# A graph attention stage's products and its edge setup: written one after the other, or in pieces between each other

## The chip, the cores and the metric

The kernel runs on one core of one Trainium2 chip. The core has five engines that run side by side: TensorE (PE, matrix products), VectorE (DVE), ScalarE (ACT), GpSimd (POOL) and SyncE (SP, which here only issues transfers). The metric is the time of one execution on the device, in microseconds (us); less is better.

## The reference, cut to what matters

Two graph layers over 6250 nodes with 256 features and 100000 edges, which come sorted by their destination. What matters here is the start of the first layer:

```python
h = jnp.maximum(_layernorm(x, axis=-1), 0.0)
Qh = (h @ Wq + bq).reshape(N, 8, 32)
Kh = (h @ Wk + bk).reshape(N, 8, 32)
Vh = (h @ Wv + bv).reshape(N, 8, 32)
s = jnp.einsum('nhc,nhc->nh', Qh, Kh) / sqrt(32)
# then, over the edges and one loop per node: a softmax by destination of leaky_relu(s[src] + s[dst]),
# a weighted sum of Vh[src], an output product, batch norm, a two-layer product, batch norm;
# then a second layer of three sums over neighbours, each with a product
```

So for each node a score per head (8) and a value row (256) are wanted before any edge can be worked on.

## The kernel before, in words

The kernel has stages that follow one another: setup of the edges, the QKV stage, attention over the edges, the two dense products with batch norm, and three stages that gather neighbours' rows. The change touches the first two, both in `gnn_kernel`.

**Edge setup** (lines 196 to 296). The edges are cut into 53 chunks of 15 x 128 places, and a chunk's edges lie in one partition at first. `srow` and `krow` (53 x 1920 and 53 x 1922, int32) are loaded from the lists of sources and destinations, `line`, `nodes`, `ahead` and `stop` for a check of the input. Then come, on VectorE if nothing else is said:

- `kf` (L234) and `base` (L238), casts to float; `loc` (L240), the destination less the chunk's first node; `sf` (L236) and `loc_h` (L242), casts on ScalarE; `loc_h` is stored by SP.
- `lst` (L245) and `fst` (L250), marks of the last and first edges of a node; `fst` is multiplied by -3e38 (L253) and stored through ScalarE's queue (`by_two`, L193).
- Three times fifteen transposes of 128 columns on TensorE (L259), of `sf`, `loc` and `lst`, eight and seven at a time into a tile `idx_tp`, and a copy of each batch (L260) into `src_t`, `loc_t` and `fst_t`, the tiles that the later stages index by chunk.
- The check (L264 to L296): two passes over `line` (125 x 800) and a dozen operations on one row; one product sums the counts, and `odd_i` receives the flag that picks the path after the QKV stage.

**QKV stage** (L299 to L344). The 6250 nodes are 50 blocks of 125 rows, in ten groups of five. A group's rows of `x` are loaded at once by SP into `xg` (two buffers). `layernorm` takes bn_stats and bn_aggr of each of the five blocks (L150, L151), then one square root on ScalarE (L141), one reciprocal and one product on VectorE (L142, L154). For each block: ScalarE makes `h0` (normalize and Relu, L320), TensorE transposes its two halves into `tp` (L323, two buffers), ScalarE copies them to `hb` (L325, three buffers) and issues its store to `h_d` (L326); TensorE multiplies `hb` with `w_qk` (L330) into `qk_ps` (two buffers) and with `w_v` (L332) into `v_ps` (one buffer). VectorE adds the biases (L334, L336), multiplies Q with K (L338) and sums by head (L341); SP stores the row `vs`, values and scores, to `vs_d` in two parts of 112 and 13 rows.

**What sets the order.** In these two stages a list scheduler picks, for each engine, what is ready by its own reckoning, with the order in the program as priority. Each engine then carries out its queue strictly in the order chosen, and an instruction that waits for a semaphore holds up all behind it on its engine; the transfers that ScalarE issues stand in ScalarE's queue. The attention stage, which isn't changed, does it otherwise: inside `tc.manual_schedule(engines={EN.PE, EN.DVE, EN.Activation})` the three engines named get their instructions in the order in which the program writes them, from a list (`PLAN`). Engines that are not named, SP and GpSimd, remain with the scheduler.

After the QKV stage all engines read the flag, and attention begins with gathers by GpSimd out of `vs_d`.

Of the kernel before, what the change touches and what calls it, by code (L numbers as in the profile page):

```python
# [29 lines left out]
I32 = mybir.dt.int32  # L30
# [57 lines left out]
def gnn_kernel(ctx: ExitStack, tc: tile.TileContext, a: dict, out: bass.AP):  # L88
# [106 lines left out]

    src, dst = a["src"], a["dst"]
    srow = cp.tile([NCK, CE], I32, name="srow")
    nc.vector.memset(srow[:, :BACK], 0)
    krow = cp.tile([NCK, CE + 2], I32, name="krow")
    nc.vector.memset(krow[:, : BACK + 1], -1)  # L200
    nc.vector.memset(krow[:, CE + 1 :], PADKEY)
    at_n = cp.tile([NCK, 1], I32, name="at_n")
    nc.vector.memset(at_n, NN - LASTW)
    for c0, c1 in ((1, 49), (49, NCK - 1)):
        at, n = c0 * STEP, c1 - c0
        nc.scalar.dma_start(srow[c0:c1, :], edges(src, at - BACK, n, CE))
        nc.sync.dma_start(krow[c0:c1, :], edges(dst, at - BACK - 1, n, CE + 2))
        nc.sync.dma_start(at_n[c0:c1, :], edges(dst, at, n, 1))
    nc.scalar.dma_start(srow[0:1, BACK:], edges(src, 0, 1, CE - BACK))
    nc.sync.dma_start(krow[0:1, BACK + 1 :], edges(dst, 0, 1, CE + 1 - BACK))  # L210
    nc.scalar.dma_start(srow[NCK - 1 :, :], edges(src, NE - CE, 1, CE))
    nc.sync.dma_start(krow[NCK - 1 :, : CE + 1], edges(dst, NE - CE - 1, 1, CE + 1))
    nc.vector.memset(at_n[0:1, :], 0)


    nc.vector.memset(nodes[:, 0:1], 0)
    nc.vector.memset(nodes[:, NCK - 1 : NCK], NN - LASTW)
    nc.vector.memset(nodes[:, NCK:], NN)
    nc.sync.dma_start(nodes[:, 1 : NCK - 1], each(dst, STEP))
    ahead = cp.tile([1, NCK], I32, name="ahead")  # L220
    nc.vector.memset(ahead[:, 0:1], -1)
    nc.sync.dma_start(ahead[:, 1 : NCK - 1], each(dst, STEP - BACK - 1))
    nc.sync.dma_start(ahead[:, NCK - 1 :], edges(dst, NE - CE - 1, 1, 1))
    stop = cp.tile([1, 1], I32, name="stop")
    nc.sync.dma_start(stop, edges(dst, STEP * (NCK - 1), 1, 1))
    line = cp.tile([125, 801], I32, name="line")
    nc.vector.memset(line[0:1, 0:1], -1)
    nc.scalar.dma_start(line[0:1, 1:], edges(dst, 0, 1, 800))
    nc.scalar.dma_start(line[1:113, :], edges(dst, 799, 112, 801, 800))
    nc.scalar.dma_start(line[113:, :], edges(dst, 799 + 112 * 800, 12, 801, 800))  # L230


    kf = cp.tile([NCK, CE + 2], FT, name="kf")
    nc.vector.tensor_copy(kf, krow)  # L234
    sf = cp.tile([NCK, CE], FT, name="sf")
    nc.scalar.copy(sf, srow)  # L236
    base = cp.tile([NCK, 1], FT, name="base")
    nc.vector.tensor_copy(base, at_n)  # L238
    loc = cp.tile([NCK, CE], FT, name="loc")
    nc.vector.tensor_scalar(loc, kf[:, 1 : CE + 1], base, None, op0=OP.subtract)  # L240
    loc_h = cp.tile([NCK, CE], BF, name="loc_h")
    nc.scalar.copy(loc_h, loc)  # L242
    by_two(nc.sync, loc_d, loc_h)
    lst = cp.tile([NCK, CK, P], FT, name="lst")
    nc.vector.tensor_tensor(  # L245
        lst.rearrange("c j e -> c (j e)"), kf[:, 2:], kf[:, 1 : CE + 1], op=OP.not_equal
    )
    nc.vector.memset(lst[:, :, P - 1 :], 1.0)
    fst = cp.tile([NCK, CK, P], FT, name="fst")
    nc.vector.tensor_tensor(  # L250
        fst.rearrange("c j e -> c (j e)"), kf[:, 1 : CE + 1], kf[:, :CE], op=OP.not_equal
    )
    nc.vector.tensor_scalar(fst, fst, -BIG, None, op0=OP.mult)  # L253
    by_two(nc.scalar, fst_d, fst)
    for of, to in ((sf, src_c), (loc, loc_c), (lst.rearrange("c j e -> c (j e)"), lst_c)):
        for j0, j1 in ((0, 8), (8, CK)):
            tp = cps.tile([P, 8, NCK], FT, name="idx_tp", bufs=2)
            for j in range(j0, j1):
                nc.tensor.transpose(tp[:, j - j0, :], of[:, j * P : (j + 1) * P], ident[:NCK, :NCK])  # L259
            nc.vector.tensor_copy(to[:, :, j0:j1].rearrange("p c j -> p j c"), tp[:, : j1 - j0, :])  # L260


    odd = cp.tile([P, 1], FT, name="odd")
    nc.vector.memset(odd, 0.0)  # L264
    fall = cp.tile([125, 800], FT, name="fall")
    nc.vector.tensor_tensor(fall, line[:, 1:], line[:, :800], op=OP.is_lt)
    nc.vector.tensor_reduce(odd[:125], fall, AX.X, OP.add)
    nodes_f = cp.tile([1, NCK + 1], FT, name="nodes_f")
    nc.vector.tensor_copy(nodes_f, nodes[:, : NCK + 1])
    ahead_f = cp.tile([1, NCK], FT, name="ahead_f")  # L270
    nc.vector.tensor_copy(ahead_f, ahead)
    bad = cp.tile([1, 3 * NCK + 2], FT, name="bad")
    nc.vector.tensor_copy(bad[:, 3 * NCK :][:, 0:1], stop)

    nc.vector.tensor_tensor(bad[:, :NCK], nodes_f[:, 1:], nodes_f[:, :NCK], op=OP.subtract)
    nc.vector.tensor_scalar(bad[:, :NCK], bad[:, :NCK], float(P), None, op0=OP.is_gt)
    nc.vector.tensor_tensor(bad[:, NCK : 2 * NCK], ahead_f, nodes_f[:, :NCK], op=OP.is_ge)
    told = cp.tile([1, NCK], FT, name="told")
    nc.vector.tensor_scalar(
        told, iota[0:1, :NCK], float(DONE[1] - DONE[0]), float(DONE[0]), op0=OP.mult, op1=OP.add  # L280
    )
    nc.vector.tensor_tensor(bad[:, 2 * NCK : 3 * NCK], nodes_f[:, :NCK], told, op=OP.is_lt)

    nc.vector.tensor_scalar(
        bad[:, 3 * NCK : 3 * NCK + 1], bad[:, 3 * NCK : 3 * NCK + 1], float(NN - LASTW), None, op0=OP.is_lt
    )
    nc.vector.tensor_scalar(
        bad[:, 3 * NCK + 1 :], nodes_f[:, NCK - 2 : NCK - 1], float(NN - P), None, op0=OP.is_gt
    )
    nbad = cp.tile([1, 1], FT, name="nbad")  # L290
    nc.vector.tensor_reduce(nbad, bad, AX.X, OP.add)
    nc.vector.tensor_tensor(odd[0:1], odd[0:1], nbad, op=OP.add)
    nodd = cps.tile([1, 1], FT, name="nodd")
    nc.tensor.matmul(nodd, odd, ones[:, 0:1], start=True, stop=True)
    odd_i = cp.tile([1, 1], I32, name="odd_i")
    nc.vector.tensor_copy(odd_i, nodd)  # L296


    with (  # L299
# [5 lines left out]
        w_v = weight(wp, "w_v", [a["L0_gnn_Wv"]])  # L305
        b_qk = wp.tile([P, 2 * D], FT, name="b_qk")
# [6 lines left out]
        for b0 in range(0, NFB, 5):  # L313
            xg = sp.tile([P, 5, D], FT, name="xg")
            halves(nc.sync, lambda s: xg[s], lambda s: rows_of(a["x"], b0, 5)[s])
            r, m = layernorm(sp, [xg[:FB, k, :] for k in range(5)], 5)
            for k in range(5):
                b = b0 + k
                h0 = sp.tile([P, D], FT, name="h0")
                nc.scalar.activation(h0[:FB], xg[:FB, k, :], AF.Relu, bias=m[:FB, k : k + 1], scale=r[:FB, k : k + 1])  # L320
                tp = pp.tile([P, 2, FB], FT, name="tp")
                for f in range(2):
# [1467 lines left out]
```

## Time and profile before

| | us |
|---|---|
| median of 14 runs | 4516.52 |
| lowest, highest | 4513.11, 4523.44 |
| the profiled execution | 4517.94 |
| its span, first to last instruction | 4516.2 |
| first product of the QKV stage starts | 30.26 |
| last group of products of the QKV stage starts | 183.40 |
| first gather of the attention stage starts | 190.89 |

A row of the order of time has the start in us, the duration in us, the engine, the line, the operation, the tiles written and read, the shapes, how many were merged, and in brackets the idle time ahead of it and what ended it. Merged rows ("x4") give the time from the first start to the last end. A matmul of this type counts twice in the records (the page's "x200" of L330 are 100 in the program). A row of the windows has, after the stretch, its length, the busy time of TensorE's matmuls, its weight loads, VectorE, ScalarE and GpSimd with their counts, the granted TensorE clock (1.00 is full), and the share and rate of the transfers. The page's rows of 40 digits are the span in equal slices of 113 us; "PEclk" is the granted clock in tenths. No clock is on record for the first 35 us; the rows show 1.00 there.

### The profile page before, as it was taken

The page shows a single profiled execution, that of the slowest core. Times are in us where ns is not written, and L with a number is a line of the kernel's source. Part 1 is how long each engine was busy: PE and PEld are TensorE (multiplying, and loading weights), DVE is VectorE, ACT ScalarE, POOL GpSimd, SP SyncE. Part 2 cuts the span into 40 slices and gives each one's busy share as a digit, 9 for nine tenths or more (in the row PEclk, how much of TensorE's full clock was granted, in tenths as well). Part 3 has the DMA queues.
Part 4 walks back from the last instruction along what each step waited for, and adds up shares of the span by engine and source line. Part 5 has one row for each costly group of instructions (what it writes and reads, how often), then busy time and mean ns, then how long its engine had stood idle before and what let it go on. Part 6 is the DMA issues. An engine that isn't in the chain of part 4 may idle for free. (4 is left out here: it accounts for less than half of the span.)

```text
span 4516.2 us, 36719 instructions
## 1 busy us (share of the span) xinstructions
PE 3647.8 (81%) x11051; PEld 1916.2 (42%) x11051; DVE 1486.1 (33%) x3034; ACT 746.1 (17%) x1610; POOL 3011.8 (67%) x3186
## 2 busy tenths in 40 slices
PE   7666666666696677888777899999999797888888
PEld 4344444444444333444333344444444333333333
DVE  6577777777724111111111121212121111111110
ACT  2244444444326000000000000000000000000000
POOL 0277777777300677777776777777776677777776
PEclk9888888888896788767777999999999656556655
DMA  4555555555205444444443777878776333333333
GB/s 126 146 150 152 152 152 153 152 152 152 69 0 159 147 126 126 126 126 126 127 126 115 221 244 231 244 232 244 232 243 205 100 112 112 112 112 112 113 112 105
DMA packets 315949, 671.18 MB, mean 149 GB/s; under 512 B 79412, under 2 KB 166734, under 8 KB 315743
## 3 DMA queue, kind: packets, MB, share of 16 engines
q0 software_dynamic: 178080, 524.47, 40.4%
q1 hardware_dynamic: 114005, 126.08, 9.2%
q10 hardware_dynamic: 23658, 18.21, 1.4%
q8 instruction: 89, 1.46, 0.1%
q14 instruction: 117, 0.96, 0.1%
HBM read 614.38 MB, written 54.13 MB: 148 GB/s over the span
## 5 line engine op out<-in xcount | busy, mean ns | idle before, releaser
L894 PE MATMUL sum<-g,hot 128*128 128x256 f32 (+1 forms) x4770 | 2276.2, 597 | 380.4 <-DMA g<-g_d,src_t 212.4
L396 POOL DMA_INDIRECT g<-g_d,src_t x1590 | 1505.6, 947 | 788.8 <-issue 522.8
L894 PEld LDWEIGHTS sum<-g,hot 128*128 128x128 f32 x4770 | 981.5, 240 | 1581.4 <-DMA g<-y_d,src_t 572.2
L396 POOL DMA_INDIRECT g<-vs_d,src_t x795 | 754.0, 948 | 431.6 <-issue 220.6
L396 POOL DMA_INDIRECT g<-y_d,src_t x795 | 751.6, 945 | 273.7 <-issue 219.5
L696 PE MATMUL acc<-g,hot 128*128 128x264 f32 x1590 | 513.9, 469 | 59.8 <-DVE g L686 58.6
L696 PEld LDWEIGHTS acc<-g,hot 128*128 128x128 f32 x1590 | 345.6, 234 | 125.2 <-DVE g L686 71.5
L413 DVE TENSOR_TENSOR hot<-ruler,loc_t 128x1920 f32<-128x1920 f32 x159 | 341.4, 2149 | 11.9 <-DMA g_d<-g 10.0
L1012 DVE TENSOR_TENSOR o<-sum,base 128x256 f32<-128x256 f32 (+1 forms) x53 | 22.5, 425 | 865.9 <-PE sum L894 865.9
L525 PE MATMUL flip<-ident,s_e 128*120 128x128 f32 x53 | 24.8, 468 | 339.5 <-ACT s_e L520 339.5
L686 DVE TENSOR_TENSOR g<-g,at_ps 128x1024 f32<-128x1024 f32 x212 | 239.2, 1150 | 15.4 <-ACT at_ps L677 9.4
L936 DVE SCALAR_TENSOR_TENSOR own<-own,eps,sum 128x256 f32<-128x256 f32 (+1 forms) x53 | 25.4, 480 | 522.2 <-PE sum L894 522.2
L966 PE MATMUL h_ps<-tt,g_w 128*128 128x512 f32 (+1 forms) x448 | 190.8, 570 | 0.6 <-ACT tt L954 0.6
L525 PEld LDWEIGHTS flip<-ident,s_e 128*120 128x120 f32 x53 | 9.3, 176 | 350.0 <-ACT s_e L520 350.0
L1000 DVE SCALAR_TENSOR_TENSOR own<-own,eps,sum 128x512 f32<-128x512 f32 (+1 forms) x53 | 39.5, 746 | 346.5 <-PE sum L894 346.5
L918 ACT COPY tt<-tp 128x256 f32<-128x256 f32 (+1 forms) x53 | 19.7, 372 | 733.0 <-PE tp L917 733.0
L925 DVE TENSOR_TENSOR g<-h_ps,g_b 128x512 f32<-128x512 f32 (+1 forms) x53 | 36.6, 691 | 305.2 <-issue 275.4
L954 ACT COPY tt<-tp 128x512 f32<-128x512 f32 (+1 forms) x53 | 31.0, 585 | 609.4 <-PE tp L953 609.4
L985 DVE SCALAR_TENSOR_TENSOR base<-y,eps,x 128x256 f32<-128x256 f32 (+1 forms) x53 | 25.5, 483 | 311.8 <-ACT y L980 310.6
L966 PEld LDWEIGHTS h_ps<-tt,g_w 128*128 128x128 f32 x448 | 82.7, 190 | 100.3 <-issue 99.5
L492 DVE TENSOR_TENSOR hot<-ruler,loc_t 128x1024 f32<-128x1024 f32 x106 | 117.2, 1145 | 5.5 <-ACT ruler L407 5.5
L506 ACT ACTIVATE hot_t<-loc_r,minus_p 128x896 bf16<-128x896 bf16 x106 | 115.6, 1091 | 9.9 <-DMA loc_r<-loc_d 9.9
(161 smaller groups left out, 2724.6 us busy)
## 6 DMA issues: line engine op xcount, KB each, us to landing
loc_r<-loc_d SPq DMA_DIRECT2D x53, 480.0 KB
g<-g_d,src_t POOLq DMA_INDIRECT x1590
g_d<-g SPq DMA_DIRECT2D x52, 256.0 KB
own<-g_d SPq DMA_DIRECT2D x52, 256.0 KB
g<-vs_d,src_t POOLq DMA_INDIRECT x795
g<-y_d,src_t POOLq DMA_INDIRECT x795
xg<-in_x_dram SPq DMA_DIRECT2D x20, 560.0 KB
own<-vs_d SPq DMA_DIRECT2D x52, 132.0 KB
```

The costliest lines, as they stand in the source:

```text
L396: nc.gpsimd.indirect_dma_start(out=to, out_offset=None, in_=table, in_offset=bass.IndirectOffsetOnAxis(ap=src_c[:, c, j : j + 1], axis=0),)
L413: nc.vector.tensor_tensor(hot, rule[:, None, :P].to_broadcast([P, CK, P]), loc_c[:, c, :][:, :, None].to_broadcast([P, CK, P]), op=OP.is_e ...
L492: nc.vector.tensor_tensor(s.hot[:, js, :], rule[:, None, :P].to_broadcast([P, n, P]), loc_c[:, s.c, js][:, :, None].to_broadcast([P, n, P] ...
L506: nc.scalar.activation(s.hot_t[:, edges_of(q)], s.loc_r[:, edges_of(q)], AF.Square, bias=minus_p)
L525: nc.tensor.transpose(s.flip[: CK * H, :P], s.s_e.rearrange("p j h -> p (j h)"), ident)
L686: nc.vector.tensor_tensor(rows, rows, s.w_e[:, j0 // 8, j0 % 8 : j0 % 8 + n, :, None].to_broadcast([P, n, H, C]), op=OP.mult,)
L696: nc.tensor.matmul(s.acc, s.hot[:, j, :], s.g[:, j, :], start=j == 0, stop=j == CK - 1)
L894: nc.tensor.matmul(ps, hot[:, j, :], g, start=j == 0, stop=j == CK - 1)
L925: nc.vector.tensor_tensor(g1[R], h_ps[R], g_b1[R], op=OP.add)
L954: nc.scalar.copy(tt[:, :, q, R], tp[:, :, R])
L966: nc.tensor.matmul(h_ps[:, :n], g_w2[:, k, f * P : (f + 1) * P], tt_f[:, k, :n], start=k == 0, stop=k == 3)
L1000: nc.vector.scalar_tensor_tensor(own[R], own[R], eps1[R, 1:2], ps[R], op0=OP.mult, op1=OP.add)
```

## The change

The edge setup becomes functions. `load_edges` holds all loads and memsets and is called after the weights, the first ten blocks of `x` and the biases have been asked for. The rest is a list of ten pieces, of which one is run after each block of products from the sixth on. `kf`, `base`, `loc` and the product of `fst` are on GpSimd. `layernorm` is taken apart: `statistics(b)` for a block of the next group stands ahead of the products of the present one, two, two and one of them in the first three blocks of a group. `turned(b + 1)` stands ahead of the products of block b. `xg` has three buffers, and SP issues the store to `h_d`. All of the loop is inside `tc.manual_schedule` for TensorE, VectorE and ScalarE.

```diff
-    (edge setup in one piece: loads, kf, sf, base, loc, loc_h, lst, fst, the transposes, the check)
+    def load_edges():
+        (all memsets and loads of srow, krow, at_n, nodes, ahead, stop, line, as before)
+    def destinations():
+        nc.gpsimd.tensor_copy(kf, krow)
+        nc.gpsimd.tensor_copy(base, at_n)
+        nc.gpsimd.tensor_scalar(loc, kf[:, 1 : CE + 1], base, None, op0=OP.subtract)
+        nc.scalar.copy(sf, srow)
+        loc_h = cp.tile([NCK, CE], BF, name="loc_h")
+        nc.scalar.copy(loc_h, loc)
+        by_two(nc.sync, loc_d, loc_h)
+    def last_edges():
+        nc.vector.tensor_tensor(lst..., kf[:, 2:], kf[:, 1 : CE + 1], op=OP.not_equal)
+        nc.vector.memset(lst[:, :, P - 1 :], 1.0)
+    def first_edges():
+        fst = cp.tile([NCK, CK, P], FT, name="fst")
+        nc.vector.tensor_tensor(fst..., kf[:, 1 : CE + 1], kf[:, :CE], op=OP.not_equal)
+        nc.gpsimd.tensor_scalar(fst, fst, -BIG, None, op0=OP.mult)
+        by_two(nc.scalar, fst_d, fst)
+    def flips(of, to):
+        (the transposes and the copy, as before; two pieces, of eight and of seven)
+    def check():
+        (as before)
+    edge_work = [
+        destinations,
+        check,
+        *flips(sf, src_c),
+        *flips(loc, loc_c),
+        last_edges,
+        *flips(lst.rearrange("c j e -> c (j e)"), lst_c),
+        first_edges,
+    ]
...
         w_qk = weight(wp, "w_qk", [a["L0_gnn_Wq"], a["L0_gnn_Wk"]])
         w_v = weight(wp, "w_v", [a["L0_gnn_Wv"]])
+        def load_x(b0):
+            xg = sp.tile([P, 5, D], FT, name="xg", bufs=3)
+            halves(nc.sync, lambda s: xg[s], lambda s: rows_of(a["x"], b0, 5)[s])
+            return xg
+        loaded = [load_x(0), load_x(5)]
...
         b_v = row(wp, "b_v", a["L0_gnn_bv"], D)
-        for b0 in range(0, NFB, 5):
-            xg = sp.tile([P, 5, D], FT, name="xg")
-            halves(nc.sync, lambda s: xg[s], lambda s: rows_of(a["x"], b0, 5)[s])
-            r, m = layernorm(sp, [xg[:FB, k, :] for k in range(5)], 5)
-            for k in range(5):
-                (h0, tp, hb, nc.scalar.dma_start to h_d, and the products)
+        load_edges()
+        mvs, norms = {}, {}
+        def statistics(b):
+            g, k = divmod(b, 5)
+            if k == 0:
+                mvs[g] = sp.tile([P, 5, 2], FT, name="ln_mv")
+            st = sp.tile([P, 6], FT, name="ln_st")
+            nc.vector.bn_stats(st[:FB], loaded[g][:FB, k, :])
+            nc.vector.bn_aggr(mvs[g][:FB, k, :], st[:FB])
+            if k == 4:
+                mv = mvs.pop(g)
+                r = rsqrt(sp, "ln_r", mv[:FB, :, 1], 5, FB)
+                m = sp.tile([P, 5], FT, name="ln_m")
+                nc.vector.scalar_tensor_tensor(m[:FB], mv[:FB, :, 0], -1.0, r[:FB], op0=OP.mult, op1=OP.mult)
+                norms[g] = r, m
+        def turned(b):
+            (h0 on ScalarE, two transposes into tp, hb on ScalarE, as before)
+            nc.sync.dma_start(h_d[:, :, b * FB : (b + 1) * FB], hb)
+            return hb
+        with tc.manual_schedule(engines={EN.PE, EN.DVE, EN.Activation}):
+            for b in range(5):
+                statistics(b)
+            nxt = turned(0)
+            for b in range(NFB):
+                g, k = divmod(b, 5)
+                for n in (2 * k, 2 * k + 1):
+                    if n < 5 and g + 1 < NFB // 5:
+                        statistics(5 * (g + 1) + n)
+                hb = nxt
+                if b + 1 < NFB:
+                    nxt = turned(b + 1)
+                if k == 4 and 5 * (g + 2) < NFB:
+                    loaded.append(load_x(5 * (g + 2)))
                 (the products of block b and VectorE's four operations, as before)
                 halves(nc.sync, lambda s: vs_d[b * FB : (b + 1) * FB, :][s], lambda s: vs[s])
+                if b > 4 and edge_work:
+                    edge_work.pop(0)()
```

Lines in brackets stand for code that is told in words.

## The prediction

> **What bounds the kernel now.** I read the page first, then the stage's waits, then its order of time, then the clock.
>
> ```profile
> span 4516.2 us, 36719 instructions
> PEclk9888888888896788767777999999999656556655
> ```
>
> The stages follow one another: GpSimd's first gather of the attention stage starts at 190.89 us, after the last products of the QKV stage, and the last matmul of that stage starts at 183.40. So whatever the QKV stage gains or loses moves the rest as a block. The profiled execution took 4517.94 us, 1.7 more than its span and 1.4 more than the median of the runs (4516.52).
>
> The stage's windows and its waits (30 to 185 us):
>
> ```profile
> 45.50:60.80 15.30, 14.81 (x51) 8.59 (x50) 11.06 (x33) 4.74 (x11) 0.00 (x0) 1.00 0.51 138
> ```
> ```profile
> PE qk_ps L330 <- ACT hb L325: 5.9, 24, 0.2
> ```
>
> In this group of five blocks TensorE is busy 14.81 of 15.30 us, VectorE 11.06, ScalarE 4.74: TensorE bounds the stage, and it waits mainly once in two blocks for a copy `hb`. The order of time gives the units:
>
> ```profile
> 27.50 0.30 ACT L141 ACTIVATE ln_r<-ln_mv,eps 125x5 f32<-125x5 f32 x1 [2.80 <-DVE ln_mv L151]
> 28.27 0.16 DVE L154 SCALAR_TENSOR_TENSOR ln_m<-ln_mv,ln_r 125x5 f32<-125x5 f32 x1
> 28.46 1.09 ACT L320 ACTIVATE h<-xg,ln_m,ln_r 125x256 f32<-125x256 f32 x2 [0.67 <-DVE ln_m L154]
> 29.12 0.29 PEld L323 LDWEIGHTS tp<-ident,h 125*128 125x128 f32 x2 [3.04 <-ACT h L320]
> 30.26 3.78 PE L330 MATMUL qk_ps<-w_qk,hb 128*125 128x512 f32 x4
> ...
> 181.68 1.88 PE L330 MATMUL qk_ps<-w_qk,hb 128*125 128x512 f32 x4
> 183.40 1.03 PE L332 MATMUL v_ps<-w_v,hb 128*125 128x256 f32 x4
> 183.59 0.69 DVE L334 TENSOR_TENSOR qk<-qk_ps,b_qk 125x512 f32<-125x512 f32 x1 [0.77 <-PE qk_ps L330]
> 184.66 0.41 DVE L336 TENSOR_TENSOR vs<-v_ps,b_v 125x256 f32<-125x256 f32 x1
> 185.00 0.41 DVE L341 TENSOR_REDUCE vs<-qk 125x8 f32<-125x256 f32 x1
> ```
>
> A block's products P take 1.72 us (181.68 to 183.40) plus 0.86 (`v` at 104.12, next transpose at 104.98) = 2.58; a block's two transposes T take 0.57 / 2 = 0.285. The scheduler's order repeats every 6.10 us for two blocks (98.67, 104.77), so 6.10 - 5.16 - 0.57 = 0.37 is waiting. The first block is slow: products from 30.26 to 35.32, 5.06 us, 2.5 over the usual.
>
> Is a written order kept even when its next instruction must wait? The attention stage has one, and there ScalarE shows:
>
> ```profile
> 460.76 0.41 ACT L772 COPY h_t<-h_own 128x256 f32 x1 [1.82 <-DVE stats L781]
> 461.07 1.04 ACT L506 ACTIVATE hot_t<-loc_r,minus_p 128x896 bf16<-128x896 bf16 x1
> ```
>
> The second has its row of `loc_r` loaded a chunk (19 us) earlier, yet stands 1.82 us behind the first, as listed. Nothing overtakes. The clock, in windows on its own grid of 3.41 us:
>
> ```profile
> 280.85:284.26 3.41, 0.23 (x3) 0.04 (x1) 3.05 (x9) 1.60 (x5) 2.61 (x3) 1.00 0.41 99
> 284.26:287.67 3.41, 0.81 (x3) 0.60 (x3) 0.90 (x3) 1.15 (x3) 2.50 (x4) 0.50 0.36 100
> 287.67:291.09 3.42, 3.42 (x16) 2.44 (x15) 2.56 (x9) 2.37 (x7) 2.54 (x3) 0.50 0.51 160
> 291.09:294.50 3.41, 2.45 (x25) 1.90 (x21) 2.80 (x8) 1.68 (x3) 2.77 (x3) 1.00 0.94 306
> ...
> 1390.18:1393.59 3.41, 1.73 (x16) 1.56 (x14) 2.06 (x6) 0.61 (x2) 0.00 (x0) 1.00 0.15 14
> 1393.59:1397.00 3.41, 1.97 (x6) 1.47 (x6) 0.65 (x4) 2.52 (x7) 0.00 (x0) 0.50 1.05 266
> ...
> 1738.34:1741.75 3.41, 2.04 (x6) 0.89 (x6) 0.00 (x0) 0.00 (x0) 2.80 (x3) 1.00 0.37 109
> 1741.75:1745.17 3.42, 1.74 (x6) 0.89 (x6) 2.02 (x2) 0.00 (x0) 2.50 (x4) 1.00 0.37 96
> ```
>
> The eighth field is the granted clock. A window with 0.23 us of TensorE work is followed by 0.50, so is one with 1.73 (a gap of 3.12 us began in it), so is 1741.75 (1.74); after 2.04 the clock held. It came back after a full window.
>
> **The change, part by part.** *Start: 13.1 us earlier.* `x` and weights now go out at 0.76 us. Traffic flowed from about 2 us and ran near 235 GB/s once queues were full (16 to 22 us: 216 to 250). The first `x` (625 KB) shares with the weights: 1.28 MB is 5.4 us, so about 8 us. Five statistics of 0.57 end near 11. But ScalarE itself issues three weight and eight edge loads ahead of its first square root, and in the run before its fourth issue went out only at 7.85, after earlier transfers had landed. Weights and `srow` (1.16 MB) with as much from SP are 10 us, so it is free near 12.1, plus the table load (1.28): 13.4. From the square root to the first product took 2.76 (27.50 to 30.26); the written order puts block 1's activation and T ahead of P(0), about 1.0 more. First product: 17.2 against 30.26. Ends: 14 and 20.
>
> *Steady order: 8.7 us less.* T(b+1) then P(b): 50 x 2.58 + 49 x 0.285 = 143.0, plus the slow first block 2.5 = 145.5. Before: 30.26 to 184.43 = 154.2. ScalarE no longer issues `h_d` (0.57 each); SP does: 0.57 + 0.32 + 0.39 for `vs_d` + 0.14 for `x` = 1.42 per block of 2.87, so it is hidden. If SP held `x` behind stores, each of eight groups would wait some 3 us (25 in all); before, `x` went out between stores, so I take nothing.
>
> *A new wait in each group: +28.8.* The fifth `statistics` of the next group stands in block k = 2 ahead of `turned(b+1)`, and contains a square root on ScalarE. So: VectorE must first finish block b-1, then bn_stats and bn_aggr; ScalarE waits with the square root; queued behind it is the activation of block b+1; TensorE waits with T(b+1), and P(b), ready, is behind that. From the end of P(b-1): 0.19 to VectorE (183.40 to 183.59), `vs` 0.41, `qk2` 0.35, reduce 0.45 = 1.40; bn_stats 0.34, bn_aggr 0.21 = 1.95; square root 0.33 = 2.28; activation 0.51 = 2.79; load 0.20 = 2.99. VectorE comes 0.2 to 0.3 late, since blocks 0 and 1 of a group carry two statistics (1.93 + 1.15 = 3.1 us against 2.87). I take 3.2, ends 3.0 and 3.5. Nine groups have a successor: 28.8.
>
> *Edge work in the stream.* It stood ahead of the products before, so its removal is in the start's term. Flips: 45 transposes of 0.117 (15 in 1.84, eight in 0.93) = +5.3 on TensorE; their copies (0.75 to 0.87) fit VectorE's slack in blocks 3 and 4. `check` after block 6: `fall` 0.96, its reduce 0.93, 14 small ones near 0.15 = 3.9, plus a matmul and a cast 0.6; it stands ahead of a k = 2 statistics, so all lengthens that wait: +4.5. `last_edges` after block 11, likewise: +2.2. `destinations`: `sf` and `loc_h` are 1.79 each on ScalarE, start 0.5 into P(5) and put the next activation at 4.5 where P ends at 2.6: +2.1. `first_edges` after block 14: reduce ends 1.40 after P, comparison 2.07, GpSimd's pass 1.85, two issues 0.62 on ScalarE's queue, behind them the activation 0.6 and 0.2: +6.8, all new.
>
> GpSimd's passes: no row shows one. iota took 232 ns for 128 columns and 127 for one, 0.83 ns a column, 1.7 us for 1920; the far end is a gather's 947 ns for 128 rows, 7.4 ns, 14.2 us. I take 1.7, an elementwise walk being nearest to iota. Then `kf` and `loc` end near 20 us, ScalarE asks at 41: hidden; at the far end they cost 3 there and 12.5 in `first_edges`. A gain is excluded, since VectorE has slack in the blocks concerned.
> The Trainium skill (GPSIMD Engine Reference, section 3.1) puts GpSimd near half of VectorE's elementwise rate, which speaks against moving work there; no run shows it, and by VectorE's 1.12 us pass it would make 2.2, 0.5 more in `first_edges`.
>
> *Clock: +19.* A gap of 3.2 us in windows of 3.41 nearly always leaves one window with over 1.6 idle, under 1.8 busy: a drop. Half clock lasts one window (loss 1.7) or two (loss up to 3.4, less the part that is gap). Averaged over where the gap falls, about 1.9. Nine groups plus `first_edges`: 10 x 1.9 = 19; ends 0 and 34.
> The Trainium skill (TensorE: Matmul & The Clock Gate, HAM oscillation) states "no PE-idle gaps >~3.4µs". By that rule nine gaps of 3.2 would be free, three long ones would drop, and the sum would be +33.6. The row at 1390.18, dropped with a gap of 3.12 us, disagrees, and I go by the row.
>
> Sum: -13.1 - 8.7 + 28.8 + 5.3 + 4.5 + 2.2 + 2.1 + 6.8 + 19 = +46.9. Against 4517.94: 4564.8, against the median 4563. After the stage nothing changes; I add nothing.
>
> **The rivals.** *The clock holds in the nine short gaps*, only those of `check`, `last_edges` and `first_edges` (6.8 to 7.7 and 5.4 us) dropping: 5.7 for 19, +33.6, 4550. For it: 1738.34 held at 2.04 busy. Against: 1390.18.
>
> *Faster: the written order doesn't bind*; T(b+1) and P(b) go ahead as they did before, where the square root (95.86) hid beside products. Then all waits (28.8 + 15.6 + 19 = 63.4) go: -13.1 - 8.7 + 5.3 = -16.5, 4500. It decides where the waits left total under 7.5 us. Against: the two ScalarE rows.
>
> *Slow feeding*: GpSimd at 14.2 us a pass (+15.5) or `x` held behind stores (+25): 4579 to 4588.
>
> **How the numbers follow.** Forecast 0.55, clock holds 0.20, slow feeding 0.12, order not binding 0.08, something about level 0.05. A measurement of this kernel tells apart about 0.2%, 9 us. Faster 0.08, same 0.04, slower 0.88. Range: from 4530 (no drop at all, 4544; start at 14 us, -3.2; gaps of 3.0, -1.8; pieces at half their 15.6, -7.8) to 4588 (slow feeding); the two lowest cases and a tail are left out.
>
> **What would show it.** First product near 17 us; last near 231 (184 before). Among the waits, TensorE's `tp` for ScalarE's `h` some 11 times, 3 us in the median and about 7 twice; ScalarE's square root <- DVE `ln_mv`, nine times near 2. The clock row under 9 in the second and third slices. The span after the stage unchanged, 4332 us. Wrong if TensorE stays busy through the blocks k = 2, or if the stage ends before 193.

## The result, and the profile after

The changed kernel takes 4560.26 us (median of 6 runs, 4558.9 to 4562.43) against 4517.15 (28 runs of the kernel before on the same chip): 1.0096 times as long, 95% interval 1.0086 to 1.0106. The forecast was 4563, slower. Its span is 4561.6 us against 4516.2, 45.4 more. From the page of the changed kernel, the span and the clock row:

```profile
span 4561.6 us, 36732 instructions
PEclk8968888888898678777788899999999665565566
```

Against the kernel before, the first slice fell from 9 to 8 tenths and the third from 8 to 6; the third begins at 228 us, behind the stage. The loss has to be sought in the first 240 us. There the stage's own marks are these (start of the first product, end of the last product, start of the first gather of the attention stage, and what is left of the span after it):

| | before | after | difference |
|---|---|---|---|
| first product | 30.26 | 25.09 | -5.2 |
| last product ends | 184.42 | 227.20 | +42.8 |
| first gather | 190.89 | 236.71 | +45.8 |
| rest of the span | 4325.3 | 4324.9 | -0.4 |

All of the loss lies ahead of the first gather. Three of the waits of the changed kernel in its first 250 us (us in total, times, longest):

```profile
PE tp L371 <- ACT h L366: 60.8, 13, 23.0
ACT ln_r L141 <- DVE ln_mv L353: 42.3, 9, 8.1
...
ACT h L366 <- POOL fst L261: 11.4, 1, 11.4
```

The copy `hb`, on which TensorE waited 24 times for 0.2 us in the kernel before, is replaced by the activation `h`, thirteen times: once at the start (23.0), the other twelve 37.8 us together. ScalarE's root waits nine times for the statistics. One such place, block 27, in order of time:

```profile
152.32 0.42 DVE L405 TENSOR_REDUCE vs<-qk 125x8 f32<-125x256 f32 x1
152.66 0.42 DVE L352 BATCH_NORM_STATS2 ln_st<-xg 125x6 f32<-125x256 f32 x1
153.11 0.18 DVE L353 BATCH_NORM_AGGREGATE ln_mv<-ln_st 125x2 f32<-125x6 f32 x1
153.32 0.30 ACT L141 ACTIVATE ln_r<-ln_mv,eps 125x5 f32<-125x5 f32 x1 [4.01 <-DVE ln_mv L353]
153.53 0.58 ACT L366 ACTIVATE h<-xg,ln_m,ln_r 125x256 f32<-125x256 f32 x1
...
154.16 0.43 PE L371 MATMUL tp<-ident,h 125*128 125x125 f32 x2 [2.67 <-ACT h L366]
```

ScalarE stood 4.01 us with the root, though the activation behind it needs only the norms of the present group, which had been there since the group before. TensorE was idle for 2.67 us. A block's period, from the start of its products to the start of the next block's, is 2.80 us where nothing stands between and 5.69 here.

The start, in order of time:

```profile
7.64 0.23 ACTq L220 DMA_DIRECT2D srow<-in_src_dram  x1
...
13.83 0.23 ACTq L222 DMA_DIRECT2D srow<-in_src_dram  x1
...
14.89 0.32 ACTq L237 DMA_DIRECT2D line<-in_dst_dram  x1
...
18.41 0.30 ACTq L238 DMA_DIRECT2D line<-in_dst_dram  x1
18.74 1.28 ACT L141 ACT_TABLE_LOAD   x1 [18.74 <-DMA krow<-in_dst_dram]
20.04 0.30 ACT L141 ACTIVATE ln_r<-ln_mv,eps 125x5 f32<-125x5 f32 x1
20.37 0.19 DVE L142 RECIPROCAL ln_r<-ln_r 125x5 f32<-125x5 f32 x1 [10.59 <-ACT ln_r L141]
20.50 1.78 POOL L242 CAST kf<-krow 53x1922 f32<-53x1922 int32 x1 [0.95 <-DMA krow<-in_dst_dram]
20.59 1.71 DVE L358 SCALAR_TENSOR_TENSOR ln_m<-ln_mv,ln_r 125x5 f32<-125x5 f32 x1
```

VectorE had been done with the statistics for 10.59 us when the root came: ScalarE's queue was held by the loads that it issues itself, at 7.64, 13.83, 14.89 and at last 18.41. Then `ln_m`, five columns, took 1.71 us instead of 0.17, until GpSimd's cast was over.

The last piece, `first_edges`:

```profile
97.03 2.14 DVE L258 TENSOR_TENSOR fst<-kf 53x1920 f32<-53x1920 f32 x1
99.26 5.05 POOL L261 TENSOR_SCALAR fst<-fst 53x1920 f32<-53x1920 f32 x1 [71.75 <-DVE fst L258]
104.34 0.69 ACTq L193 DMA_DIRECT2D fst_d<-fst  x2
105.08 0.60 ACT L366 ACTIVATE h<-xg,ln_m,ln_r 125x256 f32<-125x256 f32 x1 [11.39 <-POOL fst L261]
105.74 0.68 PE L371 MATMUL tp<-ident,h 125*128 125x125 f32 x2 [9.87 <-ACT h L366]
```

ScalarE waits with the issue of the store for GpSimd's pass of 5.05 us, the next activation is queued behind the issue, and TensorE is idle for 9.87 us.

### The profile page after: what moved, and what is told of

It reads as the page before. It is cut to its first block, busy times and chain, and to the rows that moved or that the text cites. A ratio compares the mean times of both kernels' runs of the same rounds, so it can differ in the third digit from the quotient of the medians.

```text
span 4561.6 us, 36732 instructions
## 1 busy us (share of the span) xinstructions
PE 3659.3 (80%) x11051; PEld 1921.9 (42%) x11051; DVE 1492.7 (33%) x3030; ACT 745.6 (16%) x1609; POOL 3022.7 (66%) x3190
## 4 chain that ended last, share of the span: by engine, by line
PE 34%; DMA 21%; issue 21%; POOL 18%; DVE 4%; ACT 2%; ACTq 0%; SPq 0%; POOLq 0%; DVEq 0%
POOL g L462 18%; PE sum L960 18%; DMA g<-g_d,src_t 12%; PE h_ps L1032 4%; DMA g<-vs_d,src_t 4%; DMA g<-y_d,src_t 4%; PE y_ps L1042 2%; PE ps L885 2%; PE ps L896 2%; PE acc L762 2%; PE qk_ps L394 1%; DVE g L752 1%; PE h_ps L989 1%; PE v_ps L396 1%; ACT g L926 0%
## 5 line engine op out<-in xcount | busy, mean ns | idle before, releaser
L1051 DVE SCALAR_TENSOR_TENSOR base<-y,eps,x 128x256 f32<-128x256 f32 (+1 forms) x53 | 25.6, 483 | 314.7 <-ACT y L1046 313.3
```

## The experiments

The kernel before was run on the same chip beside each of the runs below. On two of the chips everything after the QKV stage took some 1000 us more, in the kernel before too (5579.52 and 5475.97), so for five runs, marked *, the stage's own times are compared and not the totals. The stage itself takes as long there: one kernel, run on both kinds as e1 and e11, has its first gather at 202.30 and 202.20. The first product comes anywhere from 23.4 to 25.6 us in the runs whose start is that of the changed kernel, so a gain of one or two us at the first gather shows nothing. The marks of all runs, in us:

| run | first product | last ends | first gather | time against before, 95% |
|---|---|---|---|---|
| the kernel before | 30.26 | 184.42 | 190.89 | 1 |
| the changed kernel | 25.09 | 227.20 | 236.71 | 1.0096 (1.0086 to 1.0106) |
| e1_root_after | 23.57 | 193.20 | 202.30 | 1.0042 (1.0021 to 1.0062) * |
| e2_fst_by_SP | 23.37 | 217.14 | 225.73 | 1.0061 (1.0033 to 1.0088) * |
| e3_edges_by_SP | 13.63 | 218.13 | 227.34 | 1.0072 (1.0041 to 1.0103) * |
| e4_no_GpSimd | 24.43 | 224.03 | 229.58 | 1.0058 (1.0035 to 1.0082) * |
| e5_fill | 23.42 | 220.28 | 229.88 | 1.0085 (1.0068 to 1.0102) |
| e6_loads_first | 25.95 | 188.91 | 195.43 | 1.0007 (0.9997 to 1.0016) |
| e7_small_pieces | 13.38 | 172.74 | 178.73 | 0.9977 (0.9967 to 0.9987) |
| e8_four_edits | 13.81 | 185.36 | 191.63 | 1.0005 (0.9995 to 1.0015) |
| e9_pieces_moved | 13.63 | 168.06 | 174.38 | 0.9964 (0.9951 to 0.9978) |
| e10_GpSimd_beside | 25.57 | 199.99 | 206.15 | one run |
| e11_root_after_again | 23.93 | 192.95 | 202.20 | 1.0031 (1.0021 to 1.0041) |
| e12_third_x_first | 13.93 | 162.43 | 168.57 | 0.9968 (0.9942 to 0.9993) * |

The theory at the outset: four things make the loss, each an instruction that waits at the head of an engine's queue ahead of work that TensorE needs sooner. They are the root ahead of `turned(b + 1)`, the store of `fst` in ScalarE's queue, the edge loads in ScalarE's queue, and GpSimd's passes. The rival: the pieces cost their length wherever they stand, and the order matters little.

### The root behind the turn: e1_root_after, e11_root_after_again

```diff
-            if k == 4:
+        def finish(g):
                 (root, reciprocal, product, as before)
...
                     nxt = turned(b + 1)
+                if k == 2 and g + 1 < NFB // 5:
+                    finish(g + 1)
```

> The square root (with reciprocal and product) of the next group stands behind turned(b + 1) instead of ahead of it; the five bn_stats and bn_aggr stay where they are. Theory of the written order: TensorE's nine waits of 2.7 us in the blocks k = 2 go (-26.0 by the trace of the change), and with them the three clock drops that followed short gaps (about -5); the waits made by check and last_edges shrink from 4.2 and 2.2 to about half. In all -31 to -37: 4523 to 4530 us. Rival, VectorE is late because some blocks carry two statistics: the statistics are where they were, so under -5, 4555 or more.

The first gather came 34.4 us earlier than in the changed kernel, 1.5 of which are the start of this run. The same step of the group, at block 3, in order of time:

```profile
33.40 0.30 ACT L141 ACTIVATE ln_r<-ln_mv,eps 125x5 f32<-125x5 f32 x1 [1.21 <-DVE ln_mv L353]
33.61 0.58 ACT L368 ACTIVATE h<-xg,ln_m,ln_r 125x256 f32<-125x256 f32 x1
...
34.25 0.43 PE L373 MATMUL tp<-ident,h 125*128 125x125 f32 x2
```

The root still waits, 1.21 us, but the turn that it delays is one block further off: the transposes follow with no wait listed, and the period is 2.89 us instead of 5.69. The low windows of the short gaps went with them, and so did the wait and the low window behind `last_edges`. The kernel was run once more for its time as a whole:

> The kernel of e1_root_after once more, for its time as a whole: in its own stage the first gather came 34.4 us earlier than in the changed kernel. Theory (that is all it does): 4524 to 4530, 1.0017 to 1.0031 of the kernel before, so that the place of the root is over two thirds of the loss of 43 us. Rival (a part of it is given back after the stage): 4535 or more.

4529.28 us against 4515.39, ratio 1.0031 (1.0021 to 1.0041). Moving three instructions behind one call takes 0.0065 of the 0.0096, each ratio being known to 0.0010: some two thirds of the loss are the place of the root.

### The store of fst by SyncE: e2_fst_by_SP

```diff
-        by_two(nc.scalar, fst_d, fst)
+        by_two(nc.sync, fst_d, fst)
```

> The two stores of fst are issued by SP instead of ScalarE. Theory, ScalarE's queue is held by an issue that waits for GpSimd's pass: the wait of 9.9 us after block 14 goes (-10.3) and the clock drop that followed it (-2.6): 4547 us. Rival, VectorE's comparison or GpSimd itself holds TensorE there: 4558 or more.

The first gather came 11.0 us earlier, 1.7 of which are the start of this run, and the wait of 10.3 us at block 15 is gone (waits are counted here from the end of one block's products to the start of the next's, transposes included). The wait at block 17 grew from 2.94 us to 5.86. Of these 2.9 us, 1.6 are an operation of VectorE, 0.41 us elsewhere, that became long while GpSimd's pass went on (98.30 to 103.35); VectorE's comparison of 2.14 us, which stands ahead of it in the queue, is the likely rest; no run separates them.

```profile
100.12 2.00 DVE L402 SCALAR_TENSOR_TENSOR qk<-qk 125x256 f32<-125x256 f32 x1
```

### The edge loads by SyncE: e3_edges_by_SP

In `load_edges` all `nc.scalar.dma_start` become `nc.sync.dma_start`.

> All edge loads are issued by SP, none by ScalarE. Theory, ScalarE's first square root waited behind its own eight load issues (it came at 20.0 us, though its statistics were ready at 9.8): the first product moves from 25.1 to about 15 us, 4550 us. Rival, the landing of x and the weights sets the start: first product unchanged within 2 us, 4560.

```profile
10.12 0.30 ACT L141 ACTIVATE ln_r<-ln_mv,eps 125x5 f32<-125x5 f32 x1 [6.50 <-DVE ln_mv L353]
...
13.63 1.92 PE L394 MATMUL qk_ps<-w_qk,hb 128*125 128x512 f32 x2
```

With ScalarE's queue free the root follows the statistics at once, at 10.12 instead of 20.04, and the first product comes at 13.63 instead of 25.09. The first gather came 9.4 us earlier; the rest of the stage took 2.1 us longer.

### Nothing elementwise on GpSimd: e4_no_GpSimd

`kf`, `base`, `loc` and the product of `fst` go to `nc.vector`.

> kf, base, loc and the product of fst are on VectorE again, all else as in the change. first_edges gets 3.9 shorter (5.05 us on GpSimd against 1.12), ln_m 1.5 shorter (1.71 us while GpSimd's cast ran, 0.17 elsewhere), destinations about 4.3 longer (loc_h now waits for VectorE's two passes after block 5). If GpSimd's elementwise work is also what delays the first gather after the stage (9.5 us after the last product, 6.5 before the change), that falls by 3: 4556 us in all. If it has another cause, 4559 and the 9.5 us stay.

The wait of `first_edges` fell from 10.34 to 6.39 us, that of `destinations` rose from 2.03 to 6.47: there VectorE now makes `kf` and `loc` ahead of ScalarE's `loc_h`, as these rows show.

```profile
47.89 1.15 DVE L242 CAST kf<-krow 53x1922 f32<-53x1922 int32 x1
...
49.13 1.21 DVE L244 TENSOR_SCALAR loc<-kf,base 53x1920 f32<-53x1920 f32 x1
50.38 1.79 ACT L247 CAST loc_h<-loc 53x1920 bf16<-53x1920 f32 x1 [4.14 <-DVE loc L244]
```

The first gather came 7.1 us earlier, 3 more than expected. 4.0 of it lie behind the stage: the gather followed the last product by 5.5 us, as in the kernel before (6.5), where the changed kernel took 9.5. 0.7 is the start, 2.5 the stage.

### Work for TensorE in the gap: e5_fill

```diff
+                if k == 2 and g + 1 < NFB // 5:
+                    for _ in range(5):
+                        nc.tensor.matmul(fill_ps[:, D:], ident, w_v[:, 0, :], start=True, stop=True)
                 if b + 1 < NFB:
                     nxt = turned(b + 1)
```

> The changed kernel with five more products of 256 columns (unused results) on TensorE ahead of the turn of the next block in each third block of a group, where it waited 2.67 us for the root. Theory (the clock falls in windows of 3.41 us in which TensorE is idle for some 2 us or more): the nine waits stay (period 5.6 to 5.8 us), but the low windows at 36.6, 118.5 and 135.6 are gone and those behind the check and the last edges remain: the stage ends 5 to 7 us earlier than in the changed kernel. Rival (the low windows come from the long pieces of edge work alone, or the clock does not matter to these products): the same windows stay low, or they vanish and the stage ends within 1 us of 227.2.

The gaps between blocks stayed (period 5.69 us), the low windows of the short gaps are gone, and the stage from its first to its last product took 196.9 us instead of 202.1 (the first gather, with the start 1.7 us earlier in this run, 6.8). Two of the waiting places in windows of this run's clock grid (busy TensorE is the first figure after the length, the granted clock the eighth field):

```profile
31.79:35.21 3.42, 2.90 (x13) 1.88 (x12) 1.72 (x7) 1.43 (x4) 0.00 (x0) 1.00 0.38 96
35.21:38.62 3.41, 3.41 (x13) 2.02 (x12) 1.87 (x4) 1.09 (x3) 0.00 (x0) 1.00 0.52 114
110.29:113.71 3.42, 2.91 (x15) 2.25 (x14) 2.60 (x9) 0.79 (x2) 0.00 (x0) 1.00 0.28 81
113.71:117.12 3.41, 3.41 (x14) 2.04 (x13) 1.28 (x3) 1.24 (x4) 0.00 (x0) 1.00 0.38 64
```

In this run the grid lies so that, without the fill, 2.3 to 2.7 us of the gap would fall into one window at seven of the nine places; none of them dropped. So TensorE's idle time is what lowers the clock, and the clock's price, 5.2 us for the three windows, is separate from the wait's.

### The order of the loads alone: e6_loads_first

The kernel before, with the weights, ten blocks of `x` and the biases asked for ahead of the edge arrays and three buffers of `xg`; nothing else.

> The kernel before with nothing of the change but the order of the loads: weights, x of the first two groups and biases ahead of the edge arrays, x in three buffers; the edge setup stays in one piece ahead of the blocks and on VectorE, no written order. Theory (the loss is in the pieces between the blocks and in the written order, not in the loads): the first product comes up to 6 us earlier than 30.26 and the time is 4505 to 4518. Rival (the loads in this order hold back something that the blocks need): 4530 or more.

Neither the theory nor the rival: 4523.73 against 4520.83, 1.0007, no difference that can be measured. The first product came 4.3 us earlier, the last 4.5 later. The order of time says why:

```profile
25.95 3.78 PE L336 MATMUL qk_ps<-w_qk,hb 128*125 128x512 f32 x4
...
27.87 2.14 DVE L266 TENSOR_TENSOR lst<-kf 53x1920 f32<-53x1920 f32 x1
...
38.96 0.67 DVE L340 TENSOR_TENSOR qk<-qk_ps,b_qk 125x512 f32<-125x512 f32 x1
```

VectorE's setup, which stood ahead of the products before, now stands between the first products and their additions: the first addition comes 13 us after the first product. Here an earlier start was no gain, since the work that it was moved past had still to be done by the next engine in the chain.

### The four edits together: e8_four_edits

> The four edits of the first four runs together (root after the turn, fst stores by SyncE, edge loads by SyncE, no elementwise work on GpSimd), with the pieces of the change otherwise as they are. Theory (their gains of 34, 11, 9 and 7 us lie at different places and add, with a few us less where a wait moves): first gather 175 to 185, 6 to 16 us earlier than in the kernel before: 4500 to 4512. Rival (the gains overlap, one wait taking the place of another): first gather after 190, 4517 or more.

The rival held: 191.63, and 1.0005. Alone the four edits brought 34.4, 11.0, 9.4 and 7.1 us, 61.9 together (58 without the earlier starts of those runs); joined they bring 45.1. What was lost is seen block by block: `destinations`, on VectorE, makes block 6 wait 7.82 us instead of 2.03, the check still makes block 7 wait 5.51, and low windows follow at 38.7, 48.9 and 76.2. With these four places set right, pieces of 2 to 5 us still cost what the setup cost in one block ahead of the products. So the rival of the outset is wrong for the root and right for pieces of this length.

### Smaller pieces: e7_small_pieces, e9_pieces_moved, e12_third_x_first

The changed kernel with the edits of e1, e2 and e3, and the edge setup in some two dozen pieces of up to 1.3 us; the casts, the product with the constant and the copies out of PSUM on ScalarE, which is busy 9.23 of 28 us in e1's steady blocks where VectorE is busy 23.19.

```diff
+    work = {
+        4: [partial(kf_part, 0, HALF)],
+        5: [partial(kf_part, HALF, CE + 2)],
+        6: [partial(sf_part, 0, HALF)],
+        7: [partial(sf_part, HALF, CE), loc_all],
+        8: [partial(flip, sf, src_c, 0, 8), partial(lst_part, 0, HALF)],
...
-                if b > 4 and edge_work:
-                    edge_work.pop(0)()
+                for piece in work.get(b, ()):
+                    piece()
```

> What the runs so far point to, together: the changed kernel with the root after the turn of the next block, the edge loads and the stores of fst issued by SyncE, and the edge setup cut into 25 pieces of 0.6 to 1.3 us, of which ScalarE takes the casts, the product with the large constant and the copies out of PSUM, VectorE the comparisons and the check, GpSimd nothing. Theory (each wait was the length of a piece, or a root, ahead of work that TensorE needed next): first product near 14, no gap of TensorE over 1.5 us, no low window after the first blocks, last product 158 to 166 and first gather 164 to 173, which is 18 to 27 us earlier than in the kernel before: 4489 to 4500. Rival (VectorE, at 0.83 of its time busy in the steady blocks, has no room for the pieces, and the waits come back as a longer period): last product at 175 or later, 4505 or more.

4509.2 us, 0.9977 (0.9967 to 0.9987): faster than both kernels, but by its time on the rival's side; the last product, at 172.74, lies between the two. Eight gaps of 2.0 to 2.3 us remained, and one of them shows whose they are:

```profile
44.57 0.70 PE L277 MATMUL idx_tp<-ident,sf 53*128 53x53 f32 x8
...
45.31 0.87 ACT L278 CAST src_t<-idx_tp 128x424 int32<-128x424 f32 x1 [2.84 <-PE idx_tp L277]
...
45.99 0.58 ACT L391 ACTIVATE h<-xg,ln_m,ln_r 125x256 f32<-125x256 f32 x1
...
46.62 0.43 PE L396 MATMUL tp<-ident,h 125*128 125x125 f32 x2 [1.35 <-ACT h L391]
```

It was not VectorE, as the rival had it, but the same mistake once more: ScalarE waits 2.84 us at the head of its queue for transposes that stand behind TensorE's products, ahead of the activation that TensorE wants next. So the copies were put one block behind their transposes, no ScalarE piece beside a root, and `hb` got six buffers:

> e7_small_pieces with ScalarE's pieces placed anew: the copies out of PSUM one block after their transposes, none beside a root, and six buffers of hb in place of three. Theory (the eight gaps of 2.0 to 2.3 us of that run come from ScalarE, which waited at the head of its queue for the transposes, for the root or for the store of hb, ahead of the next block's h; VectorE has the room): those gaps fall to the 0.7 us of the eight transposes or to nothing, first gather 169 to 172 against 178.7, and the time is 10 to 13 us under that run's, 0.9945 to 0.9960 of the kernel before. Rival (VectorE has no room and sets the longer period): the gaps stay within 1 us of where they were, and the time within 3 us.

The gaps fell to 0.77 and 0.83 us (the transposes of a flip) or to nothing, as the theory had it, and the time to 4499.19 us, 0.9964 (0.9951 to 0.9978), 0.0004 short of its range. The first gather, 174.38, missed 169 to 172 because of a wait that had lain under the gaps: VectorE for the `x` of the third group, which SyncE issued behind the edge arrays and the stores.

```profile
36.84 0.43 DVE L382 BATCH_NORM_STATS2 ln_st<-xg 125x6 f32<-125x256 f32 x1 [6.24 <-DMA xg<-in_x_dram]
```

> e9_pieces_moved with the x of the third group loaded behind the biases and ahead of the edge arrays, and each later group one group earlier (the three buffers are all used). Theory (that run's one long wait, 6.24 us of VectorE for x at block 5, with the low window after it, is the place of that load behind the stores and the edge arrays in SyncE's queue): the wait goes, block 6 takes under 4 us, first gather 164 to 169 against 174.4, and the time is 5 to 9 us under that run's 4499 on a like chip, 0.9945 to 0.9955 of the kernel before. Rival (the edge arrays now come later, and the first pieces wait for them instead): the wait moves to kf at blocks 5 to 7, the first gather stays within 3 us of 174.4.

The wait is gone and no low window is left in the stage: first gather at 168.57, 5.8 us earlier than in e9 and 22.3 earlier than in the kernel before. The time as a whole missed its range of 0.9945 to 0.9955: the ratio on that slower chip is 0.9968, with an interval (0.9942 to 0.9993) too wide to tell whether the 22.3 us arrive in full. What is left is a smaller wait of the same queue: VectorE for a buffer of `vs`, whose store is behind the same transfers.

```profile
29.79 0.42 DVE L436 TENSOR_TENSOR vs<-v_ps,b_v 125x256 f32<-125x256 f32 x1 [3.45 <-DMA vs_d<-vs]
```

### GpSimd beside VectorE: e10_GpSimd_beside

```diff
+                if b in (24, 29, 34, 39, 43, 46):
+                    nc.gpsimd.tensor_copy(idle_b[:, :H], vs[:NCK, D:])
+                if b in (24, 29, 34):
+                    nc.gpsimd.tensor_scalar(idle_b, kf[:, :CE], -BIG, None, op0=OP.mult)
+                if b in (39, 43, 46):
+                    nc.gpsimd.tensor_copy(idle_b, srow)
```

> e1_root_after with extra passes on GpSimd (results unused) beside steady blocks: behind blocks 24, 29 and 34 the product of 53x1920 elements with a constant, behind blocks 39, 43 and 46 the cast of as many. Theory (some two-input operations of VectorE do not run beside a GpSimd pass, whatever the operands): beside the products, qk2 (0.41 us) or ln_m (0.17 us) takes 1.5 us or more, and the period of one block near each rises from 2.80 to 4 us or more; the additions that read PSUM keep their 0.68 and 0.42 us. Rival (the two long operations seen were held by something of their own places): all durations and the periods as elsewhere. The theory leaves open whether the cast does the same; beside it a duration over 1 us would say so.

GpSimd's rows of the first product and the first cast, then VectorE's beside each:

```profile
125.97 5.04 POOL L420 TENSOR_SCALAR idle_b<-kf 53x1920 f32<-53x1920 f32 x1
...
173.69 1.78 POOL L422 CAST idle_b<-srow 53x1920 f32<-53x1920 int32 x1
```
```profile
126.64 0.66 DVE L404 TENSOR_TENSOR qk<-qk_ps,b_qk 125x512 f32<-125x512 f32 x1
...
127.57 2.21 DVE L408 SCALAR_TENSOR_TENSOR qk<-qk 125x256 f32<-125x256 f32 x1
129.81 0.42 DVE L411 TENSOR_REDUCE vs<-qk 125x8 f32<-125x256 f32 x1
...
175.24 0.51 DVE L408 SCALAR_TENSOR_TENSOR qk<-qk 125x256 f32<-125x256 f32 x1
```

The theory held. Beside the three products `qk2`, both of whose inputs are in SBUF, took 2.21, 2.27 and 2.27 us instead of 0.41, and blocks 28, 33 and 38, which came to wait for it, had periods of 4.65 to 4.72; the additions that read one input from PSUM, the reduction and bn_stats kept their times. Beside the three casts it took 0.51 to 0.57, and each time it ended 0.28 to 0.29 us after the cast. By these ends it is held by the cast too, which is merely nearly over when `qk2` comes; in the changed kernel `ln_m` came at a cast's beginning and took 1.71. The Trainium skill (SBUF — State Buffer, Who interferes with whom) says that such an operation of VectorE and one of GpSimd that reads SBUF exclude each other for the whole instruction. The casts agree; beside the products VectorE's operation ended 1.23 us before the end that the profile records for GpSimd's (four places, e2's among them, all 1.23 to 1.24). Whether it was let go early or that end is recorded late, no run shows.

## Why the prediction was right

It was right in sign and main cause, and near in size; several of its terms were off. Its sum was +46.9 and the spans differ by 45.4, but that they are so near is luck: the start was 7.9 us too good and the clock 8.5 too bad, and the other errors, of both signs, nearly cancel too:

| term | predicted | measured | from |
|---|---|---|---|
| start | -13.1 | -5.2 | first product 25.09 against 30.26 |
| steady order | -8.7 | -12.0 | 49 periods of 2.80, the slow first block and the last products |
| wait for the root, nine times | +28.8 | +26.0 | 9 x (5.69 - 2.80) |
| flips | +5.3 | +4.5 | periods 3.51 to 3.58 |
| check | +4.5 | +4.2 | beyond the wait that it lengthens |
| last_edges | +2.2 | +2.2 | likewise |
| destinations | +2.1 | +2.0 | gap at block 6 |
| first_edges | +6.8 | +10.3 | gap at block 15 |
| clock | +19 | +10.5 | products longer than 2.75 us a block |
| first gather after the last product | 0 | +3.0 | 9.5 against 6.5 us |
| rest | 0 | -0.4 | span after the first gather |
| sum | +46.9 | +45.1 | |

**The order binds, and the root costs what was said.** Nine waits were foreseen in nine places with the chain that the rows show; a gap was taken at 3.2 us and is 2.67, since VectorE's `vs` follows the end of P(b-1) by 0.04 us and not 0.19, and VectorE comes no later than that. The steady blocks gained 3.3 us more than said: a block takes 2.80 us, not 2.58 and 0.285. e1 and e11 show this term together with its clock and the wait of `last_edges`, which went with it: from the first product to the first gather 32.9 and 33.4 us less than in the changed kernel. ScalarE's root waits nine times, as foreseen, but 4.0 us where nothing lengthens it, not near 2. The rival on the other side, that the written order doesn't bind, falls with them: to take its gain the order itself had to be changed. Of the rival of slow feeding nothing was seen: VectorE waits for `x` once, 5.7 us at the start, and GpSimd's pass took 5.05 us and not 14.2.

**The start was mis-sized by 7.9 us.** The prediction saw that ScalarE issues the edge loads ahead of its root, and took it to be free near 12.1 us, after 2.3 MB; the last issue stands at 18.41, and 3.62 MB had moved by 19 us. What it left out is the second five blocks of `x` and the array `line`, and that the later issues wait too, as it had seen of the fourth (7.64, 13.83, 14.89 and 18.41 are ScalarE's issues one after the other, with nothing but waiting and one short issue between them). e3, which takes the loads out of that queue, has its root at 10.12. Another 1.5 us is `ln_m` beside GpSimd's cast, a mechanism that the prediction did not have.

**GpSimd's pass was mis-sized by 3.2 us.** It took 1.85 for the product, from iota, and said that the far end was 14.2; 5.05 lies between, and this is nearly all of the error of `first_edges`. The nearest row was near for the cast (1.78) and not for the operation with a constant. VectorE's own pass of these elements takes 1.15 us in e4, so the runs show 4.4 times that. The Trainium skill (GPSIMD Engine Reference, section 3.1), by which a pass on GpSimd takes about twice VectorE's time, would have made 2.2, an estimate that these runs contradict.

**The clock was mis-sized by 8.5 us.** A drop cost 1.75 us in the mean, near the 1.9 of the forecast; six came and not ten. That a window with too little work is followed by half clock held. The limit taken from the rows of before, under 1.8 us busy, was too high for these blocks: in the QKV stages of the fourteen profiles all 35 windows at full clock in which TensorE was busy for 1.41 us or less were followed by half clock, and of the 36 with 1.43 to 2.1 all but two held (e6 and e8; both have transposes of a flip in them, as some that held have). Why the windows of before, with 1.73 and 1.74, dropped stays open. What failed besides is the average over where a gap falls in the grid. The windows of the changed kernel around the waits of blocks 2, 27 and 42:

```profile
33.15:36.56 3.41, 0.94 (x4) 0.65 (x5) 1.88 (x7) 1.26 (x4) 0.00 (x0) 1.00 0.36 96
36.56:39.97 3.41, 3.41 (x7) 1.72 (x6) 0.69 (x1) 0.39 (x1) 0.00 (x0) 0.50 0.50 96
...
149.19:152.60 3.41, 2.30 (x8) 1.11 (x6) 3.27 (x10) 0.12 (x1) 0.00 (x0) 1.00 0.26 76
152.60:156.01 3.41, 1.84 (x6) 1.02 (x7) 1.01 (x5) 1.65 (x4) 0.00 (x0) 1.00 0.15 44
156.01:159.43 3.42, 3.42 (x14) 2.09 (x13) 2.15 (x5) 0.86 (x2) 0.00 (x0) 1.00 0.47 122
...
200.40:203.81 3.41, 1.74 (x7) 0.80 (x5) 3.27 (x11) 0.00 (x0) 0.00 (x0) 1.00 0.27 80
203.81:207.23 3.42, 2.42 (x8) 1.40 (x9) 0.71 (x4) 1.65 (x4) 0.00 (x0) 1.00 0.22 65
```

The first gap (32.94 to 35.62) leaves 0.94 us of work in one window, and the next window is at half. The same gap at 151.49 is cut in two by the grid's line at 152.60, neither window is idle for over 1.6 us, and the clock holds. A group takes 16.89 us, 4.95 windows, so that the gaps drift slowly against the grid: from 151 us on all four were cut. The last of them left 1.74 us of work in a window, under the 1.8 of the forecast, and the clock held there too. So the six drops came behind the three gaps that `check`, `last_edges` and `first_edges` lengthen, and behind three of the seven short ones. The rival that the clock holds in the short gaps was thus right for four of seven, wrong for three. The second slice of the clock row, which was to fall under 9 tenths, stayed at 9. The Trainium skill (TensorE: Matmul & The Clock Gate, HAM oscillation) tolerates idle gaps up to about 3.4 us; of seven gaps of 2.67 us the three that left 0.89 to 1.36 us of work in a window dropped and the four that the grid cut held, so here it is the window and not the gap that counts.

**The time to the first gather was left out.** The prediction added nothing after the stage. In six runs in which GpSimd had made its passes more than 100 us before, it came 8.6 to 9.6 us after the last product, in the seven without passes 5.5 to 6.5; but in e10, whose last pass ended 11 us before the gather, it came after 6.2. ScalarE's first operation of the attention stage came 4.9 to 5.9 us after the last product in all fourteen, and the gather 2.9 to 4.0 us after that one in the six runs and 0.6 in the eight others: GpSimd alone is late. So the passes as such are not the cause, and what GpSimd does in those 3 us stays open.

## What to carry to other kernels

In a written order ask of each instruction that waits which instruction stands behind it on its engine and who wants that one's result; here a root one call too early cost some two thirds of the loss, an issue behind a wait (`fst_d`, the edge loads) 11.0 and 9.4 us, each taken alone, and the same fault returned unseen in the first version of the small pieces. A setup in pieces of 2 to 5 us gained nothing even with those places set right. In pieces of up to 1.3 us, many of them on ScalarE, which has more room, and each behind what it waits for, it gave 0.36%; size, engine and place were changed together there, so the runs don't say which counts for how much. Moving loads forward alone gave nothing here, since the setup then stood between the first products and their additions.

## What the runs showed of the hardware

- A pass of 53x1920 elements on GpSimd took 1.78 to 1.80 us as a cast from int32 and 5.04 to 5.17 us as an operation with a constant or a column, at every place; VectorE takes 1.12 to 1.22.
- VectorE's operations with both inputs in SBUF were held while GpSimd passed over SBUF (0.41 became 2.0 to 2.3 us, 0.17 became 1.71); those with an input in PSUM (0.66 and 0.43) and those with one input (the reduction, 0.42, and bn_stats, 0.39 to 0.42) were not.
- The granted clock went window by window on a fixed grid of 3.41 us: the same idle 2.67 us cost a window at half clock (three times) or nothing (four times), depending on whether the grid cut it. In these stages the limit lay between 1.41 and 1.43 us of work in a window, with two exceptions among 71.
